# Three edits to a graph-network kernel: where the first groups' places and B rows are loaded, and who gathers group 385

## The chip, the cores and the metric

The kernel runs on one core of one Trainium2 chip. A core has TensorE (PE in the profile, its weight loads PEld), VectorE (DVE), ScalarE (ACT), GpSimd (POOL) and SyncE (SP). The metric is the device time of one execution in microseconds (us), as the median of several runs.

## The reference

12,500 nodes with 128 features, 400,000 edges sorted by their target node `dst`, 32 features per edge. One pre-normalised message-passing layer with a GRU update:

```python
h = jnp.maximum(_layernorm(x), 0.0)
# _L0_gnn_ref(h, edge_index, edge_attr, ...):
e = jnp.concatenate([h[src], h[dst], ea], axis=-1)
m = jax.nn.relu(e @ w1 + b1) @ w2 + b2
agg = jax.ops.segment_sum(m, dst, num_segments=12500)
gi = agg @ w_ih + b_ih
gh = h @ w_hh + b_hh
r = jax.nn.sigmoid(i_r + h_r); z = jax.nn.sigmoid(i_z + h_z)
n = jnp.tanh(i_n + r * h_n)
out = x + (1.0 - z) * n + z * h
```

## The kernel before, in words

The product with `w1` is split. A = h @ w1[0:128] is made once for all nodes and stored in device memory, so that an edge needs only a gathered row of A. B = h @ w1[128:256] + b1 is made in batches and stored too. The last 32 rows of `w1` meet the edge features.

**Node stage** (to about 90 us). A loop over `q` takes chunks of four 128-row tiles of x, normalises them, transposes them into `hT_all` (h with the features on the partitions, kept on chip) and stores A. Some small work is threaded in: `setup` makes the bases of the windows, `batch_product` and `batch_store` make the first three batches of B, and `at_row` loads rows of `src`.

**Edge stage.** The 3125 tiles of 128 edges form 391 groups (`NP`) of eight tiles, and each group two units (`NU` = 782). A loop over the unit `u` writes the instructions of all engines in one order by hand. For unit u, `stages(u)` works ahead: `onehot_T(k)` compares the loaded places (`L`) with node numbers (line 586, from group 382 on line 588), three groups ahead. `pre(u+3)` is TensorE's product of `[one-hot; edge features]` with `RW[k % 4]`, which holds B rows of the two windows of group k and the weights of the features (line 683). `add` adds the gathered rows of A and applies the relu on VectorE (line 713). `seg` sums the edges into the window by a one-hot product (line 739). Every 14 groups `node` turns a block of sums into gates and output.

The loads of the edge stage are queued on SyncE: `fetch(q)` brings the places and edge features of two groups (lines 574 and 577) into a ring of three buffers `L`, `window_rows(k)` the B rows of group k (line 613). Before the unit loop stand `fetch` for q = 0, 1, 2 and `window_rows` for k = 0 to 3; their ring of buffers exists only after the node stage's buffers are given back.

**Who gathers the rows of A.** `mode` says it for each group.

- 331 groups are gathered by GpSimd, with one indirect DMA per tile (line 163), into a ring of 11 buffers. The first nine (`RAW`) take rows of x instead of A, and their h is worked out on the spot.
- 28 groups belong to ScalarE ("act") and 27 to VectorE ("dve"). Here no row of A is fetched: the engine copies columns of `hT_all`, one edge at a time, to a tile `HE_act` or `HE_dve` (line 979; line 986 with 991, two edges a step), and TensorE multiplies by `w1a` (line 694). ScalarE applies the relu of such groups (line 725).
- 5 groups belong to SyncE ("sp"), with one small DMA per edge (line 968).

A by-hand group is a job that is spread evenly over units (`run_jobs`): `START` gives the first unit, and a job of group k ends four units (sp: eight) before unit 2k. The next job of that engine follows at once.

```python
lo, hi = START[m] // 2 + 2, NP - {"dve": 5, "act": 3, "sp": 12}[m]
for i in range(n):
    k = lo + int((i + 1) * (hi - lo) / n)
```

This gives 17, 31, ..., 374, 388 for ScalarE, 22, 36, ..., 372, 386 for VectorE and 87, 160, 233, 306, 379 for SyncE.

Of the kernel before, what the change touches and what calls it, by code (L numbers as in the profile page):

```python
# [9 lines left out]
F32 = mybir.dt.float32  # L10
# [19 lines left out]
V = 32  # L30
# [25 lines left out]
SPREAD = {"dve": 27, "act": 28, "sp": 5}  # L56
START = {"dve": 14, "act": 4, "sp": 24}
NR = 12672

H_AT = 16512  # L60

# [2 lines left out]
def tile_gnn(ctx: ExitStack, tc: tile.TileContext, x, src, srcT, dstT, dstP, eaT, eaP, w1, b1, w2T, b2,  # L64
# [23 lines left out]
        return [(t0 + a * GRP + j, j, a) for j in (2 * h, 2 * h + 1) for a in range(2)  # L88
                if t0 + a * GRP + j < t1]

    mode, order = {}, {m: [] for m in SPREAD}
    for m, n in SPREAD.items():
        lo, hi = START[m] // 2 + 2, NP - {"dve": 5, "act": 3, "sp": 12}[m]
        for i in range(n):
            k = lo + int((i + 1) * (hi - lo) / n)
            while k in mode:
                k += 1
            mode[k] = m
            order[m].append(k)


    src_i = {}
# [86 lines left out]
    nc.vector.memset(brow, 0.0)  # L189
    b1b = const.tile([128, D], F32, name="b1b")  # L190
    base_d = at[96:97, :NP - 1]
    by_hand = [k for m in ("sp", "act", "dve") for k in order[m]]
    NJ = len(by_hand)
    place_of = const.tile([NJ, 2], F32, name="place_of")
    for i, (to_sp, to_others) in enumerate(((ROW, 4), (0, H_AT))):
# [107 lines left out]
    def setup(pool):  # L303
# [45 lines left out]
        yield  # L349
        place(0)  # L350

    st_all = const.tile([128, NT, 2], F32, name="st_all")
    nc.vector.memset(st_all[:, NFULL, :], 0.0)
    with tc.tile_pool(name="pp", bufs=3) as pp:
# [85 lines left out]
        for q in range(NC + 3):  # L440
            if q < NC:
                b, i0, c, e, P, n0 = chunk(q)
                if c == 0:
                    stat(b + 2)
                    fin(b + 1)
            if 1 <= q <= NC:
                b, i0, c, e, P, n0 = chunk(q - 1)
                pts[q - 1] = SEGB[q % 2]
                for j in range(c, e):
                    nc.tensor.transpose(pts[q - 1][:, (j - c) * P:(j - c + 1) * P],  # L450
                                        xs[b][:P, j, :], ident[:P, :P])
                if e == bats[b][1]:
                    load(b + 5)
            if q >= 3:
                b, i0, c, e, P, n0 = chunk(q - 3)
                if c == 0:
                    asb[b] = pp.tile([128, 8, D], F32, name="asb", bufs=2)
                nc.scalar.copy(asb[b][:P, c:e, :], pas.pop(q - 3)[:P, :e - c, :])
            if q < NC:
                b, i0, c, e, P, n0 = chunk(q)  # L460
                for j in range(c, e):
                    relu_norm(xs[b][:P, j, :], xs[b][:P, j, :], st_all[:P, i0 + j, :])
                if e == bats[b][1]:
                    sqr(b + 2)
            if 1 <= q <= NC:
                b, i0, c, e, P, n0 = chunk(q - 1)
                copy = nc.scalar.copy if q % 4 == 0 else nc.vector.tensor_copy
                copy(columns(b, c, e), pts.pop(q - 1)[:, :(e - c) * P].rearrange(
                    "f (i p) -> f i p", i=e - c))
            if q >= 4:  # L470
                for _ in range(3):
                    at_row()
            if q >= 6:
                next(setting, None)
            if q in (6, 8, 10):
                batch_product(q // 2 - 3, pp, "bt", 1)
            if q in (7, 9, 11):
                batch_store(q // 2 - 3)
            if q >= 3:
                b, i0, c, e, P, n0 = chunk(q - 3)  # L480
                if e == bats[b][1]:
                    nc.sync.dma_start(nodes(A, i0, e, P), asb[b][:P, :e, :])
            if 2 <= q <= NC + 1:
                b, i0, c, e, P, n0 = chunk(q - 2)
                pas[q - 2] = ps2.tile([128, PAIR, D], F32, name="pre")
                for j in range(c, e):
                    nc.tensor.matmul(pas[q - 2][:P, j - c, :], columns(b, j, j + 1)[:, 0, :],
                                     w1a, start=True, stop=True)
# [72 lines left out]
        nc.vector.tensor_copy(flag, f[:, 6:7])  # L561


    Ls, OH, RT, HE, SEG = ({} for _ in range(5))
    hand = {}

    def fetch(q):
        if q * QP >= NP:
            return
        n = min(QP, NP - q * QP)  # L570
        c = slice(q * QP * 512, (q * QP + n) * 512)
        Ls[q] = p3.tile([128, QP * 512], F32, name="L")
        p = dstP[:, c]
        nc.sync.dma_start(
            Ls[q].bitcast(I32)[:2 * V, :n * 512],
            bass.AP(tensor=p.tensor, offset=p.offset, ap=[list(p.ap[0]), [0, V], [1, n * 512]]))
        nc.sync.dma_start(Ls[q][2 * V:, :n * 512], eaP[:, c])

    def onehot_T(k):
        if k >= NP:  # L580
# [8 lines left out]
                                    accum_out=dlast[:2 * V, n:n + 1])  # L589


    bases = {}

    def block(k):
        return max(b for b in range(NB) if BLOCKS[b][0] <= k)

    def slot(b, i):
        return i // 2 if b < NB - 1 else (BP - BLOCKS[b][1]) // 2 + i // 2

    def window_rows(k):  # L600
        if k >= NP:
            return
        b = block(k)
        k0, n, _ = BLOCKS[b]
        if k == k0:
            _, vals = nc.values_load_multi_w_load_instructions(
                base_i[0:1, b, 0:n], engines=[ET.SP], min_val=0, max_val=4 * D * LAST,
                skip_runtime_bounds_check_because="clamped above")
            for i, v in enumerate(vals):
                bases[k + i] = v  # L610
        v = bases.pop(k)
        for a in range(2):
            nc.sync.dma_start(RW[k % 4].bitcast(U8)[V * a:V * (a + 1), a, :],
                              B_bytes[bass.ds(v + 4 * D * SHIFT * a, 4 * D * V)].rearrange(
                                  "(p f) -> p f", p=V))

    def onehot(k):
        if k >= NP or (k % 2 and k > 1):
# [330 lines left out]
    def one_by_one(m, k):  # L949
        et = {"act": ET.Activation, "dve": ET.DVE, "sp": ET.SP}[m]  # L950
        r = by_hand.index(k)
        if m == "sp":
            goal[k] = tc.alloc_semaphore(f"brought{r}"), 16 * PAIR * 128
            G[k] = pj.tile([128, GRP, 2, D], F32, name="G_sp", bufs=1)
            rows = G[k].bitcast(U8)
        else:
            hand[k] = pj.tile([128, PAIR * 128], F32, name=f"HE_{m}")
            he = hand[k].bitcast(U8)
        for e0 in range(0, PAIR * 128, LOAD[m]):
            low, high = (0, ROW * (N - 1)) if m == "sp" else (H_AT, H_AT + 4 * (N - 1))  # L960
            _, vals = nc.values_load_multi_w_load_instructions(
                at[r:r + 1, e0:e0 + LOAD[m]], engines=[et], min_val=low, max_val=high,
                skip_runtime_bounds_check_because="src holds numbers of nodes")
            if m == "sp":
                for i, v in enumerate(vals):
                    e = e0 + i
                    a, j = divmod(e // 128, GRP)
                    fetched = nc.sync.dma_start(rows[e % 128:e % 128 + 1, j, a, :],
                                                A_bytes[bass.ds(v, ROW)].rearrange("(o f) -> o f", o=1))
                    fetched.then_inc(goal[k][0], 16)  # L970
                    tc.no_tile_sem_insts.add(fetched.ins.name)
                    tc.add_to_no_dep_group(f"rows{k}", fetched.ins)
                    if i % STEP[m] == STEP[m] - 1:
                        yield
                continue
            if m == "act":
                for i, v in enumerate(vals):
                    e = e0 + i
                    nc.scalar.copy(he[:, e * 4:e * 4 + 4], column(v))  # L979
                    if i % STEP[m] == STEP[m] - 1:  # L980
                        yield
                continue
            if e0 % PIECE == 0:
                both = pj.tile([128, PIECE // 2, 4], U16, name="both")
            for i in range(0, LOAD[m], 2):
                nc.vector.scalar_tensor_tensor(both[:, (e0 % PIECE + i) // 2, :], column(vals[i + 1]),  # L986
                                               256.0, column(vals[i]), op0=ALU.mult, op1=ALU.add)
                if i % STEP[m] == STEP[m] - 2:
                    if (e0 + i + 2) % PIECE == 0:
                        p0 = e0 + LOAD[m] - PIECE  # L990
                        nc.vector.tensor_copy(  # L991
                            he[:, p0 * 4:(p0 + PIECE) * 4].rearrange("p (n c b) -> p n c b", c=2, b=4),
                            both.bitcast(U8).rearrange("p n (b c) -> p n c b", c=2))
                    yield
# [12 lines left out]
    def run_jobs(u, phase):  # L1007
        if phase == 0:
            for m, k, span in jobs.get(u, ()):
                live[m] = [one_by_one(m, k), u, span, PAIR * 128 // STEP[m], 0]  # L1010
        for m, job in list(live.items()):
            it, start, span, steps, done = job
            want = -(-steps * ((u - start) * PH + phase + 1) // (span * PH))
# [16 lines left out]
            pass  # L1030

    gathers(0)
    dst_tile(1)
    for q in range(3):
        fetch(q)
    for k in range(4):
        window_rows(k)


    def stages(u):  # L1040
# [248 lines left out]
```

## Time and profile before

| | |
|---|---|
| median of 3 runs | 3378.95 us (3376.49 to 3381.35) |
| the profiled execution | 3383.87 us, of which the span from first to last instruction is 3382.1 us |
| granted TensorE clock | 0.795 of full speed |
| busy share | PE 71%, DVE 65%, ACT 91%, POOL 75% |
| DMA | 335.77 MB, 99 GB/s on average, over 200 GB/s in the first fortieth |

A row of the costliest groups reads: line, engine, operation, what is written <- what is read, count | busy us, mean ns of one | idle time of the engine just before, and what ended it. "issue" is idle time that nothing in the profile ended. A row of the waits reads: engine, tile and line <- what ended the wait: us in total, times, longest. A row of the timeline reads: start, us, engine, line, operation, count, [idle before <- what ended it]. A row of stretches reads: from:to, length, busy us and count of each engine or of the chosen line, the granted clock, the DMA engines' share and GB/s.

### The profile page before, as it was taken

The numbers are of one execution on the slowest core, as the hardware profiler recorded it, in microseconds if no ns is written. First come the engines' busy times: TensorE is split into PE (matmuls) and PEld (weight loads), VectorE is DVE, ScalarE is ACT, GpSimd is POOL, SyncE is SP. The second block draws the span as 40 slices with busy tenths as digits, with TensorE's granted clock in tenths as the row PEclk, the third lists the DMA queues.
The fourth block names the chain that finished last, engine by engine and source line by source line (L and its number), as shares of the span: only waits on it lengthen the run. The fifth ranks groups of instructions, "written<-read, shape, count | busy, mean of one in ns | idle before, by whom it ended". The sixth has DMA issues, their size and how long they took to land. (4 is left out here: it accounts for less than half of the span.)

```text
span 3382.1 us, 93395 instructions
## 1 busy us (share of the span) xinstructions
PE 2400.4 (71%) x13113; PEld 1554.8 (46%) x13113; DVE 2213.6 (65%) x16274; ACT 3081.1 (91%) x29057; POOL 2542.8 (75%) x2654
## 2 busy tenths in 40 slices
PE   7567766776677677668776777677667767766767
PEld 6444444444444444445444444444444444444445
DVE  8566666766666666666667766666656666666665
ACT  7599899999999998998999999999889998988975
POOL 7777777777777777777777777777777777777775
PEclk9778777887888777877877878787777787778778
DMA  6433444444444444444444444444444444343332
GB/s 215 104 92 84 95 99 101 99 97 103 96 95 99 97 98 95 99 104 97 96 98 97 98 95 105 97 99 98 95 98 96 100 95 99 94 96 94 92 94 67
DMA packets 196737, 335.77 MB, mean 99 GB/s; under 512 B 69445, under 2 KB 118148, under 8 KB 196112
## 3 DMA queue, kind: packets, MB, share of 16 engines
q0 software_dynamic: 84640, 173.51, 23.0%
q1 hardware_dynamic: 111327, 156.18, 17.8%
q14 instruction: 517, 4.23, 0.4%
q8 instruction: 109, 1.79, 0.2%
q10 hardware_dynamic: 144, 0.07, 0.0%
HBM read 309.25 MB, written 20.24 MB: 97 GB/s over the span
## 5 line engine op out<-in xcount | busy, mean ns | idle before, releaser
L163 POOL DMA_INDIRECT G<-A,src_i x2576 | 2475.8, 961 | 790.4 <-issue 761.2
L979 ACT COPY HE_act<-hT_all 128x4 uint8 x28672 | 2889.0, 189 | 52.9 <-issue 29.1
L986 DVE SCALAR_TENSOR_TENSOR both<-hT_all 128x4 uint16 x13824 | 1174.3, 154 | 930.3 <-issue 925.6
L683 PE MATMUL pre<-RW,L 128*128 128x256 f32 x3128 | 1136.1, 489 | 461.3 <-DMA RW<-B 237.7
L683 PEld LDWEIGHTS pre<-RW,L 128*128 128x128 f32 x3128 | 662.8, 237 | 736.8 <-issue 420.2
L739 PE MATMUL seg<-RB,OH 128*32 128x129 f32 x6250 | 592.7, 319 | 244.2 <-DVE RB L713 211.9
L739 PEld LDWEIGHTS seg<-RB,OH 128*32 128x32 f32 x6250 | 328.0, 123 | 590.7 <-DVE RB L713 310.1
L713 DVE CUSTOM_DVE_ANT_0 RB<-pre,G 128x1024 f32<-128x1024 f32 x323 | 391.1, 1211 | 70.9 <-DMA G<-A,src_i 56.5
L586 DVE TENSOR_SCALAR L<-L,node_of 64x512 f32<-64x512 int32 x382 | 185.9, 487 | 62.2 <-DMA L<-in_dstP 59.9
L725 ACT ACTIVATE RB<-pre 128x1024 f32<-128x1024 f32 x64 | 65.0, 1016 | 91.0 <-PE pre L694 91.0
L633 DVE TENSOR_TENSOR OH<-dloc,seg 128x512 f32<-128x512 f16 (+1 forms) x198 | 132.3, 669 | 0.0
L765 PE MATMUL nd<-spot,sums 128*128 128x40 f32 x782 | 119.6, 326 | 3.6 <-DVE sums L748 3.6
L765 PEld LDWEIGHTS nd<-spot,sums 128*128 128x128 f32 x782 | 115.5, 237 | 12.7 <-issue 8.8
L991 DVE COPY HE_dve<-both 128x512 uint8<-128x512 uint8 x216 | 97.6, 452 | 7.4
L244 PE MATMUL nd<-w1b,hT_all 128*128 128x128 f32 x224 | 49.4, 368 | 73.1 <-DVE xb L850 73.1
L734 PE MATMUL seg<-zrow 1*128 1x129 bf16 x196 | 45.5, 232 | 78.1 <-DVE OH L633 78.0
L694 PEld LDWEIGHTS pre<-w1a,HE_dve 128*128 128x128 f32 x432 | 89.1, 255 | 12.4
L694 PEld LDWEIGHTS pre<-w1a,HE_act 128*128 128x128 f32 x448 | 85.9, 238 | 11.0
L694 PE MATMUL pre<-w1a,HE_dve 128*128 128x128 f32 x432 | 85.4, 333 | 0.0
L694 PE MATMUL pre<-w1a,HE_act 128*128 128x128 f32 x448 | 83.7, 319 | 0.0
L163 POOL DMA_INDIRECT G<-in_x,src_i x69 | 65.6, 950 | 21.9 <-issue 20.7
L244 PEld LDWEIGHTS nd<-w1b,hT_all 128*128 128x128 f32 x224 | 35.2, 231 | 85.5 <-DVE xb L850 80.0
(177 smaller groups left out, 1346.2 us busy)
## 6 DMA issues: line engine op xcount, KB each, us to landing
G_sp<-A SPq DMA_DIRECT2D x5120, 0.5 KB
L<-in_dstP SPq DMA_DIRECT2D x195, 256.0 KB
L<-in_eaP SPq DMA_DIRECT2D x195, 256.0 KB
G<-A,src_i POOLq DMA_INDIRECT x2576, 2.5
RW<-B SPq DMA_DIRECT2D x782, 16.0 KB
xb<-in_x SPq DMA_DIRECT2D x26, 256.0 KB
out<-xb SPq DMA_DIRECT2D x26, 256.0 KB
xs<-in_x SPq DMA_DIRECT2D x11, 512.0 KB
```

Of the source, the lines that this page charges most:

```text
L163: fetched = nc.gpsimd.indirect_dma_start(out=G[k][:, j, a, :], out_offset=None, in_=table, in_offset=bass.IndirectOffsetOnAxis(ap=src_i[c] ...
L244: nc.tensor.matmul(pm[:m, i:i + D], hT_all[:, n0 + i:n0 + i + m], w1b, start=True, stop=True)
L586: nc.vector.tensor_scalar(o, i, node_of[:, k:k + 1], None, op0=ALU.is_equal)
L633: nc.vector.tensor_tensor(p, dloc[:, e0:e1, None].to_broadcast(shape), row[:, None, :].to_broadcast(shape), op=ALU.is_equal)
L683: nc.tensor.matmul(p[:, 2 * i:2 * i + 2, :], Ls[k // QP][:, c0:c0 + 128], RW[k % 4], start=True, stop=not raw)
L694: nc.tensor.matmul(p[:, 2 * i + a, :], cols, w1a, start=False, stop=n + 1 == len(l) or l[n + 1][1] != j)
L713: made = nc.vector._custom_dve(TENSOR_ADD_SAT, out=o, in0=p, in1=G[k].rearrange("p j a f -> p (j a) f")[:, c, :], s0=float("inf"), s1=0.0)
L739: nc.tensor.matmul(p[r0:r0 + V, :D + 1], OH[k][:, a * GRP + j, :], RB[k % 2][:, 2 * j + a, :D + 1], start=False, stop=all(b != a for _, _, ...
L765: nc.tensor.matmul(p[:, bass.ds(offs[i], V + SHIFT)], sums[:, slot(b, i), :D], spot[:, i % 2, :], start=False, stop=i == len(offs) - 1)
L979: nc.scalar.copy(he[:, e * 4:e * 4 + 4], column(v))
L986: nc.vector.scalar_tensor_tensor(both[:, (e0 % PIECE + i) // 2, :], column(vals[i + 1]), 256.0, column(vals[i]), op0=ALU.mult, op1=ALU.add)
L991: nc.vector.tensor_copy(he[:, p0 * 4:(p0 + PIECE) * 4].rearrange("p (n c b) -> p n c b", c=2, b=4), both.bitcast(U8).rearrange("p n (b c) ...
```

## The change

1. `fetch` moves ahead of the node stage in the code. `fetch(0)` is called in the node stage at q = 4; it loads into a tile `HE_dve` of the by-hand pool instead of a buffer `L`, and its two DMAs go over ScalarE's queue. `fetch(1)` and `fetch(2)` follow the stage as before.
2. `window_rows(0)` to `window_rows(3)` are called in the node stage at q = 16.
3. Group 385 (`SHARED`) is no longer GpSimd's. ScalarE brings its columns 0 to 767 and VectorE columns 768 to 1023, into one tile `HE_dve`. The other by-hand groups keep their number and are respaced: ScalarE's are now 17, 30, ..., 361, 375, 385 (28 whole jobs and one of 768 columns in units 4 to 766), VectorE's 22, 36, ..., 367, 381, 385, SyncE's 85, 156, 228, 299, 371. GpSimd gathers 330 groups, among them the last five, 386 to 390.

```diff
+SHARED, CUT = NP - 6, 768
...
+    def share(m, k):
+        return (0, PAIR * 128) if k != SHARED else (0, CUT) if m == "act" else (CUT, PAIR * 128)
+
-    mode, order = {}, {m: [] for m in SPREAD}
+    mode, order = {SHARED: "both"}, {m: [] for m in SPREAD}
     for m, n in SPREAD.items():
-        lo, hi = START[m] // 2 + 2, NP - {"dve": 5, "act": 3, "sp": 12}[m]
+        lo, hi = START[m] // 2 + 2, NP - 20
+        part = 0
+        if m != "sp":
+            hi, part = SHARED, (share(m, SHARED)[1] - share(m, SHARED)[0]) / (PAIR * 128)
         for i in range(n):
-            k = lo + int((i + 1) * (hi - lo) / n)
+            k = lo + int((i + 1) * (hi - lo) / (n + part))
...
+        order[m] += [SHARED] if part else []
...
-    by_hand = [k for m in ("sp", "act", "dve") for k in order[m]]
+    by_hand = order["sp"] + order["act"] + [k for k in order["dve"] if k != SHARED]
...
     def fetch(q):
...
-        Ls[q] = p3.tile([128, QP * 512], F32, name="L")
+        if q == 0:
+            Ls[q] = pj.tile([128, QP * 512], F32, name="HE_dve")
+        else:
+            Ls[q] = p3.tile([128, QP * 512], F32, name="L")
...
+        queue = nc.scalar if q == 0 else nc.sync
...
+            if q == 16:
+                for k in range(4):
+                    window_rows(k)
+            if q == 4:
+                fetch(0)
...
-            hand[k] = pj.tile([128, PAIR * 128], F32, name=f"HE_{m}")
+            if k not in hand:
+                hand[k] = pj.tile([128, PAIR * 128], F32, name="HE_dve" if k == SHARED else f"HE_{m}")
...
-        for e0 in range(0, PAIR * 128, LOAD[m]):
+        for e0 in range(*share(m, k), LOAD[m]):
...
-                live[m] = [one_by_one(m, k), u, span, PAIR * 128 // STEP[m], 0]
+                e0, e1 = share(m, k)
+                live[m] = [one_by_one(m, k), u, span, (e1 - e0) // STEP[m], 0]
...
     gathers(0)
+    for q in (1, 2):
+        fetch(q)
     dst_tile(1)
-    for q in range(3):
-        fetch(q)
-    for k in range(4):
-        window_rows(k)
```

More of the change, by code (lines that the diff above doesn't have):

```diff
@@ L350, in setup, with fetch, block, window_rows @@
         place(0)
+    Ls = {}
+    def fetch(q):
+        if q * QP >= NP:
+            return
+        n = min(QP, NP - q * QP)
+        c = slice(q * QP * 512, (q * QP + n) * 512)
+        if q == 0:
+            Ls[q] = pj.tile([128, QP * 512], F32, name="HE_dve")
+        else:
+            Ls[q] = p3.tile([128, QP * 512], F32, name="L")
+        p = dstP[:, c]
+        queue = nc.scalar if q == 0 else nc.sync
+        queue.dma_start(
+            Ls[q].bitcast(I32)[:2 * V, :n * 512],
+            bass.AP(tensor=p.tensor, offset=p.offset, ap=[list(p.ap[0]), [0, V], [1, n * 512]]))
+        queue.dma_start(Ls[q][2 * V:, :n * 512], eaP[:, c])
+    bases = {}
+    def block(k):
+        return max(b for b in range(NB) if BLOCKS[b][0] <= k)
+    def window_rows(k):
+        if k >= NP:
+            return
+        b = block(k)
+        k0, n, _ = BLOCKS[b]
+        if k == k0:
+            _, vals = nc.values_load_multi_w_load_instructions(
+                base_i[0:1, b, 0:n], engines=[ET.SP], min_val=0, max_val=4 * D * LAST,
+                skip_runtime_bounds_check_because="clamped above")
+            for i, v in enumerate(vals):
+                bases[k + i] = v
+        v = bases.pop(k)
+        for a in range(2):
+            nc.sync.dma_start(RW[k % 4].bitcast(U8)[V * a:V * (a + 1), a, :],
+                              B_bytes[bass.ds(v + 4 * D * SHIFT * a, 4 * D * V)].rearrange(
+                                  "(p f) -> p f", p=V))
     st_all = const.tile([128, NT, 2], F32, name="st_all")
@@ L561, in check_windows @@
         nc.vector.tensor_copy(flag, f[:, 6:7])
-    Ls, OH, RT, HE, SEG = ({} for _ in range(5))
+    OH, RT, HE, SEG = ({} for _ in range(4))
     hand = {}
[L567 to L571, printed above, removed]
-        Ls[q] = p3.tile([128, QP * 512], F32, name="L")
[L573 to L577, printed above, removed]
     def onehot_T(k):
@@ L589, in onehot_T @@
                                     accum_out=dlast[:2 * V, n:n + 1])
-    bases = {}
-    def block(k):
-        return max(b for b in range(NB) if BLOCKS[b][0] <= k)
     def slot(b, i):
         return i // 2 if b < NB - 1 else (BP - BLOCKS[b][1]) // 2 + i // 2
[L600 to L615, printed above, removed]
     def onehot(k):
```

## The prediction

> **What bounds the kernel now.** I read the engines' shares first, then the costliest groups, then the waits by engine, then single stretches of the run.
>
> ```profile
> PE 2400.4 (71%) x13113; PEld 1554.8 (46%) x13113; DVE 2213.6 (65%) x16274; ACT 3081.1 (91%) x29057; POOL 2542.8 (75%) x2654
> L163 POOL DMA_INDIRECT G<-A,src_i x2576 | 2475.8, 961 | 790.4 <-issue 761.2
> POOL G L163 <- issue: 781.9, 2564, 0.3
> POOL G L163 <- PE misc L666: 3.3, 4, 2.3
> POOL G L163 <- DMA L<-in_dstP: 3.2, 1, 3.2
> ```
>
> ScalarE has the highest share, but GpSimd never stops: 2564 of its gathers begin after a gap that only their own issue ends, and that never exceeds 0.3 us. One gather costs (2475.8 + 761.2) / 2576 = 1.257 us, and a group of eight 10.05 us. Only two waits are clearly longer, 3.2 and 2.3 us, both near the start.
>
> The Trainium skill, "Perfetto Trace Analysis", section "Identifying the Most-Contended Engine", would relieve the engine of highest occupancy, which is ScalarE; this change loads it. The rows of GpSimd disagree, since its missing quarter is issue time. What the rule would give here is the first rival.
>
> The other engines, which turn a landed group into sums, I call the consumers. They run behind GpSimd at first and catch up:
>
> ```profile
> 92.84 0.94 POOL L163 DMA_INDIRECT G<-A,src_i  x1 [3.18 <-DMA L<-in_dstP]
> 203.55 1.22 DVE L713 CUSTOM_DVE_ANT_0 RB<-pre,G 128x1024 f32<-128x1024 f32 x1
> 2288.91 1.23 DVE L713 CUSTOM_DVE_ANT_0 RB<-pre,G 128x1024 f32<-128x1024 f32 x1 [0.99 <-DMA G<-A,src_i]
> DVE RB L713 <- DMA G<-A,src_i: 56.5, 27, 4.4
> 3354.97 0.94 POOL L163 DMA_INDIRECT G<-A,src_i  x1 [0.30 <-issue]
> 3361.10 1.29 DVE L713 CUSTOM_DVE_ANT_0 RB<-pre,G 128x512 f32<-128x512 f32 x2 [3.15 <-PE pre L683]
> ```
>
> The first group from A starts at 92.84 and is added only at 203.55. The first add that waits for a landing comes at 2288.91; from there the 27 waits show consumers that ride on GpSimd. The last gather starts 27.1 us before the span's end.
>
> How fast they can go when GpSimd doesn't hold them is read from 400 to 2000 us: first line 586, one instruction a group, then line 163, then all engines and the two by-hand gathers.
>
> ```profile
> 0.00:400.00 400.00, 17.36 (x35) 0.82 0.46 120
> 400.00:2000.00 1600.00, 95.24 (x195) 0.80 0.42 98
> 400.00:2000.00 1600.00, 1215.15 (x1263) 0.80 0.42 98
> sum 1600.00, PE 1141.97 PEld 725.34 DVE 1067.28 ACT 1511.69 POOL 1215.15; mean PE 285.49 PEld 181.34 DVE 266.82 ACT 377.92 POOL 303.79
> L979 ACT COPY HE_act<-hT_all 128x4 uint8 x14600 | 1467.2, 189 | 26.5 <-issue 13.9
> L986 DVE SCALAR_TENSOR_TENSOR both<-hT_all 128x4 uint16 x7136 | 605.5, 154 | 466.9 <-issue 465.3
> ```
>
> The consumers take 1600 / 195 = 8.205 us a group. GpSimd gathers 322 of the 382 groups from the ninth on, so it needs 1600 / (1263 / 8) x 322 / 382 = 8.54 us per consumed group. ScalarE is occupied 1511.69 + 26.5 = 1538 us, VectorE 1067.28 + 465.3 = 1533 us, each 96%. The consumers' margin is therefore 4%, on two nearly full engines.
>
> **The change, part by part.** *Group 385 leaves GpSimd.* Eight gathers fewer: -10.05 us on the stream that sets the end. One SyncE row load more (a 4 KB row, early, among sixty such) I cost at nothing: SyncE has waits in that stage.
>
> *ScalarE takes 768 of its columns.* One copy costs (1467.2 + 26.5) / 14600 = 0.102 us, so 78.6 us more work, and 28.75 groups in units 4 to 766 instead of 28 in 4 to 772: one per 13.25 consumed groups instead of 13.71. Per ScalarE group 104.8 us go to copies and (1511.69 - 1467.2) / 195 = 0.23 us per consumed group to all else. Its load per consumed group rises from 104.8 / 13.71 + 0.23 = 7.87 to 104.8 / 13.25 + 0.23 = 8.14 us. In its order behind these copies stand the relu of by-hand groups and the gates' sigmoids, for which TensorE waits.
>
> *VectorE takes 256 columns.* 128 steps at (605.5 + 466.9) / 7136 = 0.150 us are 19.2 us; its load per consumed group rises from 7.86 by under 1% to about 7.93. Groups of SyncE end 8 groups earlier at 3% more density; its row waits are among what the consumers' pace already holds.
>
> *The consumers' new pace* no row shows. Floor: both loads, 8.14 and 7.93, stay under 8.205 and hide, so 8.205. Ceiling: the 8.205 - 7.89 = 0.32 us that the pace now stands above ScalarE's occupied time (1538 / 195) stays on top: 8.14 + 0.32 = 8.45. The nearest rows are the five stretches from 400 us to 2200 us in which ScalarE's jobs already had only 13 groups (line 586 again):
>
> ```profile
> 495.70:602.80 107.10, 6.12 (x13) 0.78 0.43 99
> ...
> 2069.50:2174.60 105.10, 6.34 (x13) 0.82 0.41 98
> sum 535.70, DVE 31.00; mean DVE 6.20
> ACT RB L725 <- PE pre L694: 91.0, 26, 12.4
> ACT gt L824 <- PE nd L818: 63.3, 19, 9.0
> ```
>
> 535.7 / 65 = 8.24 us a group, although ScalarE was as dense there as it will be. A single dense stretch can lean on the looser one after it, so I put the sustained pace a little higher, at 8.30. ScalarE's 154 us of waits for TensorE are slack it can give up.
>
> *The start.* Places of groups 0 and 1 and B rows of groups 0 to 3 come during the node stage.
>
> ```profile
> 90.21 0.66 SPq L574 DMA_DIRECT2D L<-in_dstP  x1
> 90.92 0.55 SPq L577 DMA_DIRECT2D L<-in_eaP  x1
> 100.32 0.48 DVE L586 TENSOR_SCALAR L<-L,node_of 64x512 f32<-64x512 int32 x1 [9.76 <-DMA L<-in_dstP]
> 100.40 24.35 SPq L613 DMA_DIRECT2D RW<-B  x10
> 118.39 1.19 PE L683 MATMUL pre<-RW,L 128*128 128x256 f32 x2 [11.73 <-DMA RW<-B]
> 124.86 0.94 POOL L163 DMA_INDIRECT G<-A,src_i  x1 [2.34 <-PE misc L666]
> 3302.49 0.73 DVE L588 TENSOR_SCALAR_CACHE_REDUCE L<-L,node_of 64x512 f32<-64x512 int32 x1
> ```
>
> The waits of 9.76 and 11.73 us stand in series; I let the consumers begin 17 of these 21.5 us earlier, since two more loads of places still follow the stage. Of that the end gets only GpSimd's wait for a raw group's buffer, 2.34 - 0.30 = 2.0 us; the rest is a lead of the consumers. The two loads now issue on ScalarE (0.66 + 0.55 = 1.2 us on SyncE), in a stage with gaps; eight B-row issues go ahead of at most two stores of A on SyncE.
>
> The Trainium skill, "DMA: Bandwidth & Descriptors", section "Issuing engines are not separate DMA queues", says that a second issuing engine saves only the issuing time. By that the queue alone is worth 1.2 us of lead and none of the end; the lead comes from the moment of issue, which a free buffer allows.
>
> **Sum.** 10.05 + 2.0 = 12.1 us off: 3383.87 to 3371.8 for the profiled execution, span 3370.0. It ran 4.9 us over the median, 3378.95, so the median goes to 3366.9.
>
> This holds if the consumers are through in time. The row at 3302.49 places group 383 (line 588 serves 382 to 390; it is the second), 79.6 us before the end; group 35 stood at 400. With the lead the consumers' own end is 400 - 17 + 348 P + 79.6 = 463 + 348 P at a pace P. At 8.30 that is 3351, 19 us inside. They reach GpSimd's end at P = 8.353, today's end at 8.388.
>
> **Rivals.** *ScalarE becomes the bound (slower).* At the ceiling, 8.45, the end is 463 + 348 x 8.45 = 3404, 21.5 us over today's span: 3400. It decides from P = 8.388, 2.2% above today's pace, where ScalarE's load rises by 3.4%. For it: both engines at 96%. Against: the five dense stretches at 8.24.
>
> *Gain given back.* P between 8.36 and 8.40: the consumers end level with today, -7 to +7 us, about 3379.
>
> *Node stage longer.* The early half megabyte and SyncE's eight issues push the last stores of A. GpSimd's 3.18 us wait at 92.84 is for them, so each us costs one. With 4 us: 3370.9. Were it shorter instead, up to 2.9 us more would be gained: 3364.0.
>
> **How the numbers follow.** Forecast 0.52, ScalarE as bound 0.27, given back 0.13, longer node stage 0.08. A difference of 0.2% (6.8 us) is about what can be told here. Faster: 0.52, three quarters of the node-stage case (0.06) and none of the second: 0.58; same 0.15; slower 0.27. The range goes from 3361 (the shorter wait and 3 us of the last add's wait for TensorE) to 3399, almost at the ceiling.
>
> **What would show it.** Right: 2637 gathers by GpSimd in all, none with a wait for a buffer; the first places within about 91 us, no wait of 11 us before the first L683; waits of VectorE for landings near the end; ScalarE at about 3160 us busy. Wrong: no add that waits for a landing after 2300 us, GpSimd waiting for VectorE's adds (buffers), TensorE or VectorE waiting for ScalarE's relu, and a pace of line 586 above 8.35 us a group.

## The result, and the profile after

The changed kernel takes 3389.43 us (median of 8 runs, 3386.89 to 3394.29) against 3380.59 us of before in the same session: ratio 1.003, 95% interval 1.002 to 1.004. It is slower by about 0.3%, where 0.4% faster was forecast. The profiled execution took 3389.88 us, its span is 3388.0 us.

The page of after: engines, and the gathers.

```profile
PE 2399.1 (71%) x13129; PEld 1540.9 (45%) x13129; DVE 2218.8 (65%) x16403; ACT 3165.7 (93%) x29826; POOL 2532.4 (75%) x2646
L171 POOL DMA_INDIRECT G<-A,src_i x2568 | 2465.3, 960 | 793.5 <-issue 763.2
```

The waits of after:

```profile
POOL G L171 <- issue: 783.9, 2571, 0.3
PE pre L702 <- DMA RW<-B: 300.7, 82, 10.1
ACT gt L843 <- PE nd L837: 47.8, 10, 8.3
ACT RB L744 <- PE pre L713: 24.6, 11, 5.1
POOL G L171 <- DMA L<-in_dstP: 10.8, 1, 10.8
```

GpSimd lost its eight gathers at the old price, (2465.3 + 763.2) / 2568 = 1.257 us each, and waits for no buffer. But the row "DVE RB <- DMA G", 56.5 us in before, is gone: no add waits for a landing any more. The consumers never meet GpSimd. TensorE's waits for B rows grew from 237.7 to 300.7 us. ScalarE's own waits for TensorE halved, as if its load were the matter; the experiments below tell how far that is true.

The timeline of after, from several windows: the first gather from A, the first add, the placing of groups 35 and 230 (numbered from 0; line 627 is before's 586), the last gather.

```profile
100.45 0.94 POOL L171 DMA_INDIRECT G<-A,src_i  x1 [10.79 <-DMA L<-in_dstP]
190.29 1.22 DVE L732 CUSTOM_DVE_ANT_0 RB<-pre,G 128x1024 f32<-128x1024 f32 x1
395.24 0.47 DVE L627 TENSOR_SCALAR L<-L,node_of 64x512 f32<-64x512 int32 x1
2025.68 0.51 DVE L627 TENSOR_SCALAR L<-L,node_of 64x512 f32<-64x512 int32 x1
3347.54 0.94 POOL L171 DMA_INDIRECT G<-A,src_i  x1 [0.30 <-issue]
```

GpSimd starts on A 7.6 us later than before, yet its last gather starts 7.4 us earlier, 3347.54 instead of 3354.97. From there to the end it was 27.1 us; now it is 40.5 us. The consumers began 13.3 us earlier (first add at 190.29 instead of 203.55) and were slower on the way: (2025.68 - 395.24) / 195 = 8.361 us a group, against (2005.26 - 405.35) / 195 = 8.205 us in before. I call this quotient, group 35 to group 230, the pace.

### The profile page after: what moved, and what is told of

Its sections match the earlier page's. It is cut to its first block, busy times and chain, and to the rows that moved or that the text cites. A ratio compares the mean times of both kernels' runs of the same rounds, so it can differ in the third digit from the quotient of the medians.

```text
span 3388.0 us, 94354 instructions
## 1 busy us (share of the span) xinstructions
PE 2399.1 (71%) x13129; PEld 1540.9 (45%) x13129; DVE 2218.8 (65%) x16403; ACT 3165.7 (93%) x29826; POOL 2532.4 (75%) x2646
## 3 DMA queue, kind: packets, MB, share of 16 engines
q1 hardware_dynamic: 111183, 155.66, 17.3%
## 5 line engine op out<-in xcount | busy, mean ns | idle before, releaser
L171 POOL DMA_INDIRECT G<-A,src_i x2568 | 2465.3, 960 | 793.5 <-issue 763.2
L702 PE MATMUL pre<-RW,L 128*128 128x256 f32 x3112 | 1137.0, 492 | 445.6 <-DMA RW<-B 300.7
L784 PE MATMUL nd<-spot,sums 128*128 128x40 f32 x782 | 109.6, 310 | 2.3 <-DVE sums L767 2.3
L784 PEld LDWEIGHTS nd<-spot,sums 128*128 128x128 f32 x782 | 105.4, 219 | 10.5 <-issue 7.7
L713 PEld LDWEIGHTS pre<-w1a,HE_act 128*128 128x128 f32 x448 | 83.1, 231 | 10.2
L833 PE MATMUL nd<-DEG,brow 34*128 34x512 f32 (+2 forms) x112 | 66.5, 675 | 26.7 <-ACT gt L843 26.0
L713 PEld LDWEIGHTS pre<-w1a,HE_dve 128*128 128x128 f32 x448 | 78.6, 219 | 8.9
L999 ACT COPY HE_dve<-hT_all 128x4 uint8 x768 | 77.1, 189 | 1.4 <-issue 0.8
L713 PE MATMUL pre<-w1a,HE_dve 128*128 128x128 f32 x448 | 77.1, 300 | 0.0
```

What stands on the lines that cost most here:

```text
L171: fetched = nc.gpsimd.indirect_dma_start(out=G[k][:, j, a, :], out_offset=None, in_=table, in_offset=bass.IndirectOffsetOnAxis(ap=src_i[c] ...
L702: nc.tensor.matmul(p[:, 2 * i:2 * i + 2, :], Ls[k // QP][:, c0:c0 + 128], RW[k % 4], start=True, stop=not raw)
L713: nc.tensor.matmul(p[:, 2 * i + a, :], cols, w1a, start=False, stop=n + 1 == len(l) or l[n + 1][1] != j)
L784: nc.tensor.matmul(p[:, bass.ds(offs[i], V + SHIFT)], sums[:, slot(b, i), :D], spot[:, i % 2, :], start=False, stop=i == len(offs) - 1)
L833: nc.tensor.matmul(pg, brow[:, c], DEG[:, :w], start=True, stop=False)
```

## Experiments

All were timed beside before in their own session. "Pace" is read from one profiled execution each; kernels with the same lists of by-hand groups agree in it within 0.005 us (8.205 and 8.201; 8.361, 8.358 and 8.356). The waits in the last column are those of the whole run.

| kernel | us, before beside it | ratio and 95% interval | pace, us | PE waits for RW, us |
|---|---|---|---|---|
| before | | | 8.205 | 237.7 |
| after | 3389.43, 3380.59 | 1.003, 1.002 to 1.004 | 8.361 | 300.7 |
| prologue_only_b | 3384.76, 3380.19 | 1.0014, 1.0004 to 1.0023 | 8.201 | 207.7 |
| share_only_b | 3397.51, 3380.19 | 1.0056, 1.0040 to 1.0073 | 8.358 | 297.6 |
| fetch0_sync_b | 3384.49, 3380.19 | 1.0020, 1.0010 to 1.0030 | 8.356 | 335.4 |
| act_thin_b | 3376.59, 3380.19 | 0.9989, 0.9980 to 0.9999 | 8.348 | 298.3 |
| sp_respaced | 3398.74, 3379.94 | 1.0055, 1.0037 to 1.0073 | 8.368 | 453.8 |
| act_respaced | 3379.97, 3379.94 | 1.0000, 0.9991 to 1.0010 | 8.213 | 259.1 |
| dve_respaced | 3374.48, 3379.94 | 0.9985, 0.9976 to 0.9995 | 8.303 | 214.8 |
| sp_shifted_b | 3383.24, 3384.55 | 1.0000, 0.9989 to 1.0012 | 8.289 | 322.8 |
| after_sp_sparse_b | 3369.20, 3381.50 | 0.9964, 0.9950 to 0.9978 | 8.207 | 90.7 |

### The two halves of the change

*prologue_only_b*: after with before's `mode` and `order`, so only the early loads.

```diff
-SHARED, CUT = NP - 6, 768
+SHARED, CUT = -1, 768
...
-    mode, order = {SHARED: "both"}, {m: [] for m in SPREAD}
+    mode, order = {}, {m: [] for m in SPREAD}
...
-        lo, hi = START[m] // 2 + 2, NP - 20
+        lo, hi = START[m] // 2 + 2, NP - {"dve": 5, "act": 3, "sp": 12}[m]
         part = 0
-        if m != "sp":
-            hi, part = SHARED, (share(m, SHARED)[1] - share(m, SHARED)[0]) / (PAIR * 128)
```

> The early loads alone, by-hand groups as before. Theory (before is bound by GpSimd, after by the consumers): line 586's instruction keeps about 8.2 us a group until the consumers meet GpSimd, VectorE's waits for landings are there again from before 2300 us on, and the time follows GpSimd's start on A, 7.7 us later, less 2 us of buffer wait: 5 to 6 us slower than before. Rival (the consumers bind before too): their earlier start shows in the end, 8 to 12 us faster than before.

It came out 4.6 us slower, near the 5 to 6 us of the theory. Its waits and its last gather:

```profile
DVE RB L730 <- DMA G<-A,src_i: 71.9, 36, 5.7
```
```profile
3359.71 0.94 POOL L169 DMA_INDIRECT G<-A,src_i  x1 [0.30 <-DMA G<-A,src_i]
```

36 adds wait for landings, and the last gather starts 4.7 us later than in before. So before follows GpSimd, and the early loads alone cost what they cost GpSimd.

*share_only_b*: after with the first loads where before has them, behind the node stage and on SyncE's queue.

```diff
...
-            if q == 16:
-                for k in range(4):
-                    window_rows(k)
-            if q == 4:
-                fetch(0)
...
-    for q in (1, 2):
-        fetch(q)
     dst_tile(1)
+    for q in range(3):
+        fetch(q)
+    for k in range(4):
+        window_rows(k)
```

> Group 385 and the new spacing alone, loads behind the node stage as before. Theory (the consumers bind at about 8.39 us a group): they start 12.7 us later than in after, so about 3400 us, 18 us slower than before. Rival (the late A rows cost the time): GpSimd starts on A at 92.8 us again, so about 3380 us, level with before.

17.3 us slower, with the pace of after. Its last gather starts at 3340.90, 14 us earlier than before's, and helps nothing. The loss sits in the second half of the change, and the consumers' earlier start pays part of it back.

*fetch0_sync_b*: the queue alone.

```diff
-        queue = nc.scalar if q == 0 else nc.sync
+        queue = nc.sync
```

> After, with the early places on SyncE's queue. Theory (SyncE's second store of A waits 10.2 us for a landing on the other queue): that wait goes, the first gather from A starts at 93 to 95 us, the consumers start 6 to 8 us earlier than in after and end 6 to 8 us earlier, about 3382 us. Rival (the half megabyte holds up the stage whatever the queue): first gather near 100 us, time as after.

A miss on the stage: the first gather from A starts at 98.71, not at 93 to 95. SyncE's wait of after and of this kernel:

```profile
SPq L535 <- DMA HE_dve<-in_dstP: 10.2, 1, 10.2
```
```profile
SPq L471 <- DMA HE_dve<-in_dstP: 7.4, 1, 7.4
```

On its own queue SyncE waits too, 7.4 us at a later load. Its time is 5 us under after's in the medians, but the two intervals overlap. What holds up the node stage is mostly the early half megabyte, not the queue that it comes over: in after, SyncE's load of x at 67.86 us already stands 6.9 us behind its place in before (60.99), and only then, at 73.46, do the eight B rows begin. No run has one without the other.

### ScalarE's load

*act_thin_b* writes, in every job of ScalarE, one of 32 edges as a copy of its neighbour, so one copy in 32 is left out.

```diff
-                    nc.scalar.copy(he[:, e * 4:e * 4 + 4], column(v))
+                    if e % 32 == 30:
+                        nc.scalar.copy(he[:, e * 4:e * 4 + 8].rearrange("p (n b) -> p n b", b=4),
+                                       column(v)[:, None, :].to_broadcast([128, 2, 4]))
+                    elif e % 32 != 31:
+                        nc.scalar.copy(he[:, e * 4:e * 4 + 4], column(v))
```

> After, but ScalarE leaves out one of 32 edges of each job (its neighbour's row is written twice by one instruction): 3.1% fewer copies, as many per consumed group as before. Theory (ScalarE's load sets the pace): the pace falls from 8.39 to about 8.2 us a group, waits for landings return, GpSimd sets the end, about 3375 us. Rival (VectorE's load or SyncE's denser row loads set it): within 4 us of after, no waits for landings.

The time came out as expected and the reason did not. Set against before, it is 12 us better than after, but the pace is 8.348 us, not 8.2, and no add waits for a landing. Group 35 is placed at 394.2 us, group 230 at 2022.0, group 383 at 3302.6, where after has 395.2, 2025.7 and 3312.9: two thirds of the gain came after group 230. Had only the time been read, ScalarE's load would have passed as the cause of the pace. It isn't, so the theory of these first runs fell, and the three new lists were tried one at a time.

### Which list

Each puts one new list into before, and all other places stay; group 385 stays GpSimd's. The edit is the same in all three, here SyncE's:

```diff
+    given = {"sp": [85, 156, 228, 299, 371]}
...
-            k = lo + int((i + 1) * (hi - lo) / n)
+            k = given[m][i] if m in given else lo + int((i + 1) * (hi - lo) / n)
```

> Before, with only SyncE's five groups at the new places 85, 156, 228, 299, 371. The pace is read from group 35 to group 230 (8.205 us in before, 8.361 in after, 8.348 with ScalarE's copies cut by 3.1%). Theory A (SyncE's denser row loads hold up the B rows): pace 8.33 to 8.37 and waits of TensorE for RW near 300 us instead of 238; time about 10 us over before. Theory B (the places of ScalarE's or VectorE's groups): pace 8.2, time within 3 us of before.

> Before, with only ScalarE's 28 whole groups at the new places (17, 30, 43, ..., 361, 375), 13.26 groups apart instead of 13.74; group 385 stays GpSimd's. Theory B1 (ScalarE's denser jobs set the pace of after): 8.33 to 8.37 us from group 35 to group 230, time about 10 us over before. Rivals (SyncE's or VectorE's places): pace 8.2, time within 3 us of before.

> Before, with only VectorE's 27 groups at the new places (22, 36, 50, 64, 77, ..., 367, 381): no longer every 14 groups in step with the blocks of nodes, and 1% denser. Theory B2 (VectorE's load, or the lost step with the blocks, sets the pace of after): 8.33 to 8.37 us from group 35 to group 230, time about 10 us over before. Rivals (ScalarE's or SyncE's places): pace 8.2, time within 3 us of before.

SyncE's list alone makes before 18.8 us slower, more than twice the loss of the whole change. ScalarE's list, 3.6% denser, costs nothing. VectorE's makes it 5.5 us faster although its pace is 8.303: its last gather starts at 3351.12 and the end follows 21.5 us later; no experiment tells why. Neither its theory (8.33 to 8.37) nor its rivals (8.2) had that pace, and SyncE's list cost twice the 10 us that its theory gave. The placing of group 383, in the order SyncE's, ScalarE's, VectorE's list, shows which of them delays the consumers over the whole run (before: 3302.49):

```profile
3315.36 0.73 DVE L589 TENSOR_SCALAR_CACHE_REDUCE L<-L,node_of 64x512 f32<-64x512 int32 x1
3288.99 0.73 DVE L589 TENSOR_SCALAR_CACHE_REDUCE L<-L,node_of 64x512 f32<-64x512 int32 x1
3283.31 0.72 DVE L589 TENSOR_SCALAR_CACHE_REDUCE L<-L,node_of 64x512 f32<-64x512 int32 x1
```

Only SyncE's does. The row of sp_respaced that carries the verdict, and its placing of groups 35 and 230:

```profile
PE pre L684 <- DMA RW<-B: 453.8, 113, 11.2
```
```profile
405.93 0.49 DVE L587 TENSOR_SCALAR L<-L,node_of 64x512 f32<-64x512 int32 x1
2037.64 0.47 DVE L587 TENSOR_SCALAR L<-L,node_of 64x512 f32<-64x512 int32 x1
```

TensorE waits 453.8 us for B rows, in 113 places instead of 66. No add waits for a landing, so the consumers set this end too. But the 18.8 us can't all be put down to the list, because GpSimd was late in this kernel as well:

```profile
L164 POOL DMA_INDIRECT G<-A,src_i x2576 | 2486.1, 965 | 791.1 <-issue 762.1
```

Each gather took 965 ns instead of 961, and the last one starts at 3366.00, 11.0 us later than in before and 28.8 us ahead of the end. So even consumers at before's pace would have ended late here, near 3393 us with the 27.1 us that before takes after its last gather. Why the gathers were slower is open. It is the pace that speaks against the list, and share_only_b, which has after's pace, lost 17.3 us with an early GpSimd.

The B rows stand in SyncE's queue behind its one-row loads. The timeline of SyncE in after shows how full that queue is:

```profile
1299.75 0.82 SPq L396 DMA_DIRECT2D RW<-B  x2
1300.66 7.30 SPq L988 DMA_DIRECT2D G_sp<-A  x16
1308.13 0.81 SPq L396 DMA_DIRECT2D RW<-B  x2
1309.06 0.59 SPq L373 DMA_DIRECT2D L<-in_dstP  x1
1309.71 0.50 SPq L376 DMA_DIRECT2D L<-in_eaP  x1
1310.33 5.29 SPq L988 DMA_DIRECT2D G_sp<-A  x16
1316.69 0.35 SPq L774 DMA_DIRECT2D xb<-in_x  x1
1317.15 0.87 SPq L396 DMA_DIRECT2D RW<-B  x2
```

From the B rows of one group to those of the next it is 8.38 us, and SyncE is at work all the time: two B rows, sixteen single rows and, inside the 7.30 us, one load of the next 32 row numbers into registers (line 981, 2.13 us). Then with two loads of places and one of x, 9.02 us. In before the queue is as full at the same place:

```profile
1291.39 0.81 SPq L613 DMA_DIRECT2D RW<-B  x2
1294.46 5.11 SPq L968 DMA_DIRECT2D G_sp<-A  x16
1299.74 0.82 SPq L613 DMA_DIRECT2D RW<-B  x2
```

That is 8.35 us, with the register load (2.09 us) in the gap. From 400 to 2000 us the waits of SyncE's queue add up to 86 us in before and 88 us in after, 5% of the stretch. So before stood at the edge of its SyncE queue already.

My reading is that the consumers' pace is the time that SyncE's queue takes for a group. It rests on sp_respaced and on the thinner loads below, not on a row of after. From 400 to 2000 us, where the pace is read, TensorE's waits for B rows are these, in before, after, sp_respaced and the thinned kernel of the next section:

```profile
PE pre L683 <- DMA RW<-B: 184.4, 51, 9.4
PE pre L702 <- DMA RW<-B: 187.1, 54, 8.9
PE pre L684 <- DMA RW<-B: 265.1, 61, 10.5
PE pre L703 <- DMA RW<-B: 63.6, 23, 8.1
```

Before and after wait alike there. What grew in after is TensorE's waiting for VectorE's adds (products and sums together), from 162.6 to 189.2 us. How SyncE's and VectorE's lists share the loss of after is therefore open: no kernel with after's other two lists and SyncE's old one was timed beside a before of 3380 us.

### Thinner row loads

*after_sp_sparse_b* is fetch0_sync_b with SyncE's jobs stretched to 140 to 144 units.

```diff
-START = {"dve": 14, "act": 4, "sp": 24}
+START = {"dve": 14, "act": 4, "sp": 10}
...
+    given = {"sp": [80, 156, 232, 309, 384]}
```

> After with the early places on SyncE's own queue (that kernel alone took 3384.5 us) and SyncE's jobs thinned: groups 80, 156, 232, 309, 384, the first from unit 10, so 140 to 144 units each instead of 132 to 138. Theory (SyncE's queue is full, and the density of its row loads sets the consumers' pace): under 8.25 us from group 35 to group 230 (8.356 there), waits for landings return, GpSimd sets the end: 3363 to 3373 us, faster than both kernels. Rival (ScalarE's added load binds once SyncE doesn't): pace 8.3 or more, the end still the consumers', 3378 us or more.

3369.20 us, 12.3 us faster than the before beside it (ratio 0.9964), where fetch0_sync_b was 4.3 us slower than its own. Of its page, its waits, and its timeline (groups 35 and 230, last gather):

```profile
PE 2418.3 (72%) x13129; PEld 1551.4 (46%) x13129; DVE 2222.6 (66%) x16403; ACT 3157.4 (94%) x29826; POOL 2532.6 (75%) x2646
```
```profile
PE pre L703 <- DMA RW<-B: 90.7, 30, 8.5
DVE RB L733 <- DMA G<-A,src_i: 27.1, 10, 4.3
```
```profile
393.61 0.47 DVE L628 TENSOR_SCALAR L<-L,node_of 64x512 f32<-64x512 int32 x1
1994.04 0.47 DVE L628 TENSOR_SCALAR L<-L,node_of 64x512 f32<-64x512 int32 x1
3345.77 0.94 POOL L172 DMA_INDIRECT G<-A,src_i  x1 [0.30 <-issue]
```

With 3 to 9% more units for each of SyncE's jobs, the waits for B rows fall from 335.4 to 90.7 us and the pace to 8.207, with every copy of ScalarE's added load in place. Landings are waited for again, and the end comes 21.0 us after the last gather. SyncE's queue at the same place:

```profile
1300.20 0.81 SPq L397 DMA_DIRECT2D RW<-B  x2
1307.71 0.82 SPq L397 DMA_DIRECT2D RW<-B  x2
1310.78 5.13 SPq L989 DMA_DIRECT2D G_sp<-A  x16
1316.07 1.24 SPq L397 DMA_DIRECT2D RW<-B  x2
1323.28 0.82 SPq L397 DMA_DIRECT2D RW<-B  x2
```

The B rows follow each other at 7.51, 8.36 and 7.21 us. The gap after 1307.71 is no room: it is a load of row numbers again (2.08 us). But the queue's waits from 400 to 2000 us rise from 88 to 110 us. ScalarE is occupied there for 1577.9 of 1600 us (1553.38 busy and 24.5 before its copies), so it is likely the next to bind.

*sp_shifted_b* asks whether density alone did it.

```diff
-START = {"dve": 14, "act": 4, "sp": 24}
+START = {"dve": 14, "act": 4, "sp": 20}
...
+    given = {"sp": [85, 158, 231, 304, 377]}
```

> Before, with SyncE's five groups two earlier (85, 158, 231, 304, 377) and the first job four units earlier, so that each job keeps its 142 or 136 units. Theory (density of the row loads): pace 8.2 us from group 35 to group 230 as in before (8.205), time within 4 us of before. Rival (where the jobs fall against the blocks of nodes and the other by-hand groups): pace 8.3 or more, time 10 us or more over before, as with the five new places (8.368, 19 us over).

Between the two. The time is that of before, as density has it, but the pace is 8.289 and TensorE waits 322.8 us for B rows: moving SyncE's groups two earlier at equal density costs 0.084 us of pace, half of what its new list costs (0.163). It costs no time here; adds wait for landings again (14 of them, 26.2 us), so the end is GpSimd's. So where the jobs fall matters as well as how dense they are; how the two divide stays open.

### Runs in other sessions

Nine of the runs fell into sessions in which before itself took 5735 to 5739 us; they are compared only with that. There the profile of prologue_only shows long gaps before ScalarE's copies:

```profile
L997 ACT COPY HE_act<-hT_all 128x4 uint8 x28672 | 3165.4, 189 | 2188.1 <-issue 2158.6 <-remote 1.2 <-ACT HE_act L997 0.7
L169 POOL DMA_INDIRECT G<-A,src_i x2576 | 2461.8, 956 | 3062.8 <-DVE RB L730 2163.9 <-issue 702.6 <-remote 88.9
```

2158.6 us of ScalarE's idle time lie in gaps before its copies that nothing but issue ends, where prologue_only_b, the same kernel, has 38.2 us, and GpSimd waits 2163.9 us for buffers. The granted clock was 0.668 instead of 0.796. The consumers bind there. Ratios there: prologue_only 0.9998 (0.9980 to 1.0017), share_only 1.0175 (1.0154 to 1.0196), fetch0_sync 1.0184 (1.0161 to 1.0206), act_thin 1.0048 (1.0030 to 1.0066), after_sp_old (after with SyncE's list of before) 1.0204 and, again, 1.0184, sp_shifted 0.9977, sp_sparse (before with SyncE's thinner jobs) 0.9990, after_sp_sparse 1.0195.

What was expected of these runs, in the order in which they were made. The first four are the kernels of the sections above with the same names:

> Only the early loads are kept; the by-hand groups and their spacing are those of before. Theory (after was bound by the consumers, before by GpSimd): the pace of line 586's instruction stays near 8.2 us a group, waits of VectorE for landings return near the end, and the time follows GpSimd, which starts on A 7.7 us later (100.5 instead of 92.8 us) and saves 2 us of buffer wait: 5 to 6 us slower than before. Rival (the consumers bound both kernels): their start 12.7 us earlier is worth most of that: 8 to 12 us faster than before.

> Only group 385 and the new spacing are kept; the loads stand after the node stage as before. Theory (the consumers bound it at about 8.39 us a group): the consumers start 12.7 us later than in after and end as much later: about 18 us slower than before, 12 us slower than after. Rival (the late A rows cost the time): GpSimd starts at 92.8 us again and the kernel is 8 us faster than after, level with before or better.

> After, but the early places go over SyncE's queue. Theory (SyncE's store of A waited 10.2 us for the landing on the other queue): this wait goes, the first gather from A starts at 93 to 95 us, the consumers start 6 to 8 us earlier too, and the end, which is theirs, comes 6 to 8 us earlier than in after. Rival (the half megabyte itself holds up the stage): first gather still near 100 us, time as after within 2 us.

> After, but of every 32 edges of a ScalarE job one is left out (its neighbour's row is written twice by one instruction), so that ScalarE makes 3.1% fewer copies, about as many per consumed group as before. Theory (ScalarE's load set the pace): the pace falls from 8.39 to about 8.2 us a group, waits for landings return, and the end follows GpSimd: 12 to 16 us faster than after. Rival (VectorE's load or SyncE's denser row loads set it): within 4 us of after, no waits for landings.

Then the kernels on SyncE's list:

> After, with only SyncE's five groups back at 87, 161, 233, 306, 379 (160 is VectorE's now), so about 136 units for each instead of 133. Theory (SyncE's queue is full, and the density of its row loads sets the consumers' pace): 8.2 to 8.25 us from group 35 to group 230, waits for landings return, GpSimd sets the end: 3366 to 3374 us. Rival (the three new lists together cost it): pace 8.33 or more, 3383 us or more.

> Before, with SyncE's five groups two earlier (85, 158, 231, 304, 377) and the first job four units earlier, so that each job keeps its 142 or 136 units. Theory (density): pace 8.2 as in before, time within 4 us of before. Rival (where the jobs fall against the blocks of nodes and the other by-hand groups): pace 8.3 or more, time 10 us or more over before, as with the five new places.

> Before, with SyncE's first job at unit 10 instead of 24 and its groups at 80, 156, 231, 308, 384, so that each has 140 to 144 units, 4% more than before. Theory (SyncE's full queue sets the pace): 8.0 to 8.13 us from group 35 to group 230; the end stays GpSimd's, 0 to 8 us under before. Rival (place, or other engines): pace 8.2 or more.

> After, with SyncE's jobs as thin as that (80, 156, 232, 309, 384, first one at unit 10) and the early places on SyncE's own queue. Theory: pace under 8.25 us, waits for landings return, GpSimd sets the end: its last gather starts near 3346 us, the end comes 17 to 27 us later, 3363 to 3373 us, faster than both kernels. Rival (ScalarE's load binds once SyncE doesn't): pace 8.3 or more and the end still the consumers', 3378 us or more.

> After, with only SyncE's five groups back at 87, 161, 233, 306, 379 (160 is VectorE's now). Theory (SyncE's queue is full, and the density of its row loads sets the consumers' pace): 8.2 to 8.25 us from group 35 to group 230 (8.361 in after), waits for landings return, GpSimd sets the end: 3366 to 3374 us. Rival (the three new lists together, ScalarE's added load among them, cost it): pace 8.33 or more, 3383 us or more.

There ScalarE's load looks like the price: the kernels with group 385 by hand lose 1.8 to 2%, whatever SyncE's list, and with 3.1% fewer copies 0.5%. The expectations were written for a before of 3380 us and are not decided by these runs; after_sp_old was not seen beside such a before. after_sp_sparse_b is the nearest to it, but with a thinner list than before's. Why issue is so slow in those sessions stays open.

## Why the prediction was wrong, point by point

**GpSimd's stream: right.** One gather at 1.257 us, 2637 gathers in all (2568 and 69 raw ones), no wait for a buffer. With the late start added, -10.05 - 2.0 + 7.6 gives -4.5 us for the last gather; it was -7.4.

**The condition that the consumers be through: right in form, failed in size.** The formula counted groups at a pace and a fixed tail. In after, group 35 stood at 395.2 us, 348 groups to group 383 took 8.384 us each, and 75.1 us came after it: together the span, 3388.0. Two terms ahead of the pace were off. Group 35 of before was put at 400 and stands at 405.35, and the lead was put at 17 us and was 12.7 us at group 5 (130.5 instead of 143.2) and 10.1 at group 35. With 395.24 in place of 383 the consumers reach GpSimd's forecast end at a pace of 8.319 and today's end at 8.354, not at 8.353 and 8.388. At the forecast 8.30 they would still have ended at 3363, inside GpSimd's 3370, so it was the pace that decided. "Gain given back" had the right pace (8.36 to 8.40) but not the time, for want of that lead.

**The step that failed: the pace.** The prediction costed the pace from ScalarE's and VectorE's loads, took 8.30, and dismissed the third term in half a sentence: "Groups of SyncE end 8 groups earlier at 3% more density; its row waits are among what the consumers' pace already holds." The ground given, that the pace already held these waits, doesn't stand: SyncE's queue had 5% of its time left, and a denser list of row loads slowed the pace. Put into before alone, SyncE's list takes the pace from 8.205 to 8.368, as much as the whole change does, while ScalarE's takes it to 8.213; thinning SyncE's loads takes the changed kernel back to 8.207. VectorE's load, costed at "under 1%", isn't shown to hide either: its list alone gives 8.303 up to group 230, though group 383 then comes earlier than in before. The sign was in the rows of before: TensorE's largest wait at line 683 was "DMA RW<-B", 237.7 us, and such a wait can come from a full issuing queue. The page counts no DMA issue as busy, so SyncE has no share in its first section, and the prediction shows SyncE's queue only up to the first groups. The floor, 8.205, was all but reached in after_sp_sparse_b (8.207); the dense stretches at 8.24 were a fair guide to ScalarE's load and said nothing of SyncE's.

**The rival "ScalarE becomes the bound": right side, wrong engine.** The consumers did bind, 8.361 to 8.384 against its 8.45. But ScalarE's new list alone cost 0.0 us, and with SyncE's jobs thin ScalarE ran at 94% and the kernel was 12 us faster than before. Its load isn't free in after: taking 3.1% off brought about 12 us back, mostly after group 230. The rule of the Trainium skill ("Perfetto Trace Analysis", "Identifying the Most-Contended Engine") pointed to the engine of highest occupancy. By act_respaced, which loads it 3.6% more densely and costs 0.0 us, that engine was not the bound of before.

**The start.** The two waits of 9.76 and 11.73 us went and the consumers got 12.7 of the 17 us. "Node stage longer" came true with 7.6 us, twice the 4 us of that rival, and fetch0_sync_b shows that it comes on either queue. By the Trainium skill ("DMA: Bandwidth & Descriptors", "Issuing engines are not separate DMA queues") a second issuing engine saves only the issuing time. The trace agrees in that nothing more was saved: the first gather started at 100.45 with the second queue and at 98.71 without it.

**The range** ended at 3399 and held the time, which is luck: that width was there for ScalarE as the bound. The chance went to the wrong side, 0.58 for faster.

## What to carry to other kernels

Before an engine's load is raised by a few per cent, list every in-order stream that the pace hangs on, the queue that only issues DMAs among them, and read it from its timeline: whether issue follows issue with no room between. A wait for a small load that is asked for groups ahead can be a sign of a full queue: here such waits fell from 335.4 to 90.7 us when the queue was thinned. Read such waits in the stretch where the pace is read, too; the total of a run can grow elsewhere. An experiment that brings the time back is no proof of a cause until the quantity that the cause acts on has moved too.

## What the hardware showed that was not expected

One load of 256 KB in the node stage, issued at 22.79 us, released a waiting store of SyncE only at 36.83 us, 14 us later, from either queue with a like effect (10.2 and 7.4 us of wait). And one program (prologue_only_b and prologue_only) took 3384.76 and 5739.77 us in different sessions, with ScalarE's 28672 copies 189 ns long in both, and with 38.2 us of gaps before them that only issue ends in the one and 2158.6 us in the other.
